# A decoder's last expert layer: gathered rows get buffers of their own, the one-hot rows are made in two blocks, the row maps go ahead of the last shared expert, and an activation table is loaded early

## The chip, the cores and the metric

The kernel runs on one core of a Trainium2 chip. The metric is the time of one execution in device microseconds (us); for each kernel the median of several runs is given. A core has five engines that run beside each other and wait for each other through semaphores: PE (matrix products and transposes), DVE (elementwise work and reductions), ACT (functions and copies), POOL (here mostly the issue of indirect DMAs, which gather or scatter rows by an index), and SP (the issue of plain DMAs). Each engine executes its own list of instructions in order.

## What is computed

The reference is a two-layer decoder on 1024 tokens of 256 numbers. The first layer is a decayed linear attention, a token-hashed expert layer and a layer that retrieves rows of a table. The second is a block-local attention, a quantised cross attention and an expert layer. Only the last one is touched by the change; it is, shortened:

```python
shared_output = _swiglu(x, shared_w1, shared_w3, shared_w2)
scores = jax.nn.sigmoid(x @ gate_w.T)
_, topk_idx = jax.lax.top_k(scores + bias, 2)              # 2 of 16 experts
sel = jnp.take_along_axis(scores, topk_idx, axis=1)
combine = jnp.zeros((T, E)).at[jnp.arange(T)[:, None], topk_idx].add(sel / sel.sum(-1, keepdims=True))
for e in range(E):
    y = _swiglu(x, w1[e], w3[e], w2[e])                    # silu(x w1') * (x w3') w2', inner size 176
    routed_output = routed_output + combine[:, e:e + 1] * y
x = x + shared_output + routed_output                      # x in the experts is layernorm(x)
```

## The kernel before, in words

The tokens lie in eight tiles of 128. Everything up to the row maps is written as Python generators ("streams") that a small planner, `Clock.weave` (lines 117 to 148), interleaves. A stream yields the engine that it needs next; the planner keeps an estimated free time per engine and takes the stream that could start first, where a stream's `lead` is subtracted from that start. `fork` (line 150) starts sub-streams with the lead of their parent. What comes out is one fixed order on each of PE, ACT and DVE. POOL's and SP's orders, and everything after line 1326, are set by the framework's own scheduler. Because a planner's helper records every operation, all of these have line 77 in the profile and are told apart by the names of their tiles.

The last layer is handled tile by tile by `route` (line 1142): layernorm, gate logits, the two best experts of each token as one-hot rows `oh`, and `rank`, each token's position among the tokens of its expert. The normalised rows are stored to DRAM as `xs` (line 366). For the last tile, number 7, line 1177 forks three sub-streams:

- `maps` (line 1234) works out, for up to 31 slots of 128 rows, which token row each slot row gathers (`smap`), where its result goes (`rmap`), and which expert the slot belongs to (`te`). It counts slots with a scan, builds `cols`, and then 16 times makes a 128x128 one-hot block `ohs` on DVE (lines 1275 and 1276, four buffers) and multiplies it with a slice of `cols` on PE (line 1278), all into one accumulator `pmap`. After that come `part0`, `rmap`, `smap`, then `past`, `tef`, `te`, then `none` and a last correction of `rmap`.
- `gates` (line 1182), five small DVE instructions, gives the weights `gsel` that are used at the very end.
- `shared` (line 1194) is the shared expert of tile 7: two products with `s13` (PE), tanh (ACT), two products (DVE, `hd6`), transposes (PE), copies (ACT, `hT6`), two products with `s2` (PE), and the sum into `x7` (DVE).

Then the pools of those streams are closed, a pool `work_c` is opened in the same memory (line 1329), and `run` (line 1377) goes over 24 slots, with 7 more only if they are used. For slot i, `up` (line 1338) loads the expert's number from `te` into a register of PE, gathers 128 rows of `xs` by `smap` with an indirect DMA into `xr` (four buffers of `work_c`, line 1342), transposes them on PE (`tpx`), copies to `xrT` on DVE, makes `ph` on PE (two products of 128x352, in four passes), Silu on ACT and a product on DVE (`hd`). `down` (line 1359) transposes `hd` (`tph`), copies it (`hT`, one part on ACT and one on DVE), makes `py` on PE, copies it to `yr` on ACT, and scatters the rows to `ys` in DRAM (line 1372). The end reads `ys` back, weighs and adds (lines 1394 to 1400).

Two more places matter. `free` (line 864) closes the first layer's pools and opens in their memory the pool `w2` (routed weights, and the maps) and above it `wb2` and `work2` (the last layer's small weights and work tiles). And the loads of those weights (`w_wp` to `w_w2b`, lines 870 to 878) stand in SP's list among the loads `hb` (line 676) that feed the table retrieval.

Of the kernel before, what the change touches and what calls it, by code (L numbers as in the profile page):

```python
# [11 lines left out]
F32 = mybir.dt.float32  # L12
BF16 = mybir.dt.bfloat16
I32 = mybir.dt.int32
U32 = mybir.dt.uint32
U8 = mybir.dt.uint8
AF = mybir.ActivationFunctionType
ALU = mybir.AluOpType
AX = mybir.AxisListType
PSUM = bass.MemoryType.PSUM  # L20

P = 128
D = 256
NT = 8
# [14 lines left out]
NE, EI = 16, 176  # L39
NSL = 2 * NT + NE - 1  # L40
# [4 lines left out]
def bc(ap, axis, n):  # L45

    shape = list(ap.shape)
    shape.insert(axis, n)
    return ap.unsqueeze(axis).to_broadcast(shape)


class Clock:
# [94 lines left out]
                s.done = self.end  # L147
            s.t = self.end + self.HOP * (s.wait[0] != self.last)

    def fork(self, *gens):  # L150

        made = [Stream(g, self.lead, self.end + self.HOP, self.rank) for g in gens]
        self.live.extend(made)
        yield "vector", lambda: max(s.done for s in made) if all(s.done is not None for s in made) else None

# [49 lines left out]
def decoder(ctx, tc, a, out):  # L205
# [3 lines left out]
    ck = Clock(nc)  # L209
# [7 lines left out]
    A = SimpleNamespace(turned=None, freed=None)  # L217
# [646 lines left out]
    def free():  # L864

        yield "vector", lambda: None if fronts_left or A.turned is None else max(A.turned, *known.values())
        front_ctx.close()
        w2 = ctx.enter_context(tc.tile_pool(name="w2", bufs=1))
        wb = work_ctx.enter_context(tc.tile_pool(name="wb2", bufs=1))
        A.wp = load(wb, "wp", [P, 2, D], rows("wp"))  # L870
        A.bp_b = load(wb, "bp", [P, D], a["bp"].to_broadcast([P, D]))
        A.gate = load(wb, "gate", [P, 2, NE], rows("gate"))
        A.gbias = load(wb, "gbias", [P, NE], a["gbias"].to_broadcast([P, NE]))
        A.s13 = load(wb, "s13", [P, 2, 2 * EI], rows("s13"))
        A.s2a = load(wb, "s2a", [P, D], a["s2"][0:P, :])
        A.s2b = load(wb, "s2b", [EH, D], a["s2"][P:EI, :])
        A.w2a = load(w2, "w2a", [P, NE, D], a["w2"][:, 0:P, :].rearrange("e p n -> p e n"))
        A.w2b = load(w2, "w2b", [EH, NE, D], a["w2"][:, P:EI, :].rearrange("e p n -> p e n"))
        A.work2 = work_ctx.enter_context(tc.tile_pool(name="work2", bufs=1))
        A.w2 = w2  # L880
        A.one16 = A.work2.tile([P, NE], F32, name="one16", tag="one16")
        nc.vector.memset(A.one16, 1.0)
        A.spare = A.work2.tile([P, NSL], F32, name="spare", tag="spare")
        nc.gpsimd.iota(A.spare, pattern=[[P, NSL]], base=2 * (P + T), channel_multiplier=1,
                       allow_small_or_imprecise_dtypes=True)
        A.ohr = A.work2.tile([P, NT, 2, NE], F32, name="ohr", tag="ohr")
        A.freed = ck.end
        yield "vector", None
# [253 lines left out]
    def route(*tiles):  # L1142
        work = A.work2
        n, t0 = len(tiles), tiles[0]
        xnT = work.tile([P, 2, n * P], F32, name="xnT6", tag="xnT6")
        yield from layernorm_T(work, "r", tiles, xnT, store=xs)
        pl = yield from bank.take([P, n, NE])
        for i in range(n):
            for k in range(2):
                te_.matmul(pl[:, i, :], xnT[:, k, i * P:(i + 1) * P], A.gate[:, k, :], start=(k == 0), stop=(k == 1))  # L1150
        yield "scalar", None
        sg = work.tile([P, n, NE], F32, name="sg", tag="sg")
        se_.activation(sg, pl, AF.Exp, scale=-1.0)
        bank.give(pl)
        yield "vector", None
        ve_.tensor_scalar(sg, sg, 1.0, None, ALU.add)
        ve_.reciprocal(sg, sg)
        rt = work.tile([P, n, NE], F32, name="rt", tag="rt")
        ve_.tensor_tensor(rt, sg, bc(A.gbias, 1, n), ALU.add)
        for i, t in enumerate(tiles):  # L1160
            m8 = work.tile([P, 8], F32, name="m8", tag="m8", bufs=2)
            ve_.max(m8, rt[:, i])
            i8 = work.tile([P, 8], U32, name="i8", tag="i8", bufs=2)
            ve_.max_index(i8, m8, rt[:, i])
            ve_.tensor_tensor(oh[:, t], bc(i8[:, 0:2], 2, NE), bc(iota16, 1, 2), ALU.is_equal)
            ve_.tensor_tensor(took[:, t, :], oh[:, t, 0, :], oh[:, t, 1, :], ALU.add)
            ve_.tensor_tensor(prior[:, t + 1, :], prior[:, t, :], took[:, t, :], ALU.add)
            yield "tensor", None
        prk = yield from bank.take([P, n, NE])
        for i, t in enumerate(tiles):  # L1170
            te_.matmul(prk[:, i, :], lower, took[:, t, :], start=True, stop=False)
            te_.matmul(prk[:, i, :], ones, prior[:, t, :], start=False, stop=True)
        yield "scalar", None
        se_.copy(rank[:, t0:t0 + n, :], prk)
        bank.give(prk)
        if t0 + n == NT:
            yield from ck.fork(maps(), gates(tiles, sg), shared(tiles, xnT))
        else:
            yield from gates(tiles, sg)
            yield from shared(tiles, xnT)  # L1180

    def gates(tiles, sg):
        work, n, t0 = A.work2, len(tiles), tiles[0]
        yield "vector", None
        sw = work.tile([P, n, 2, NE], F32, name="sw", tag="sw")
        gs = gsel[:, t0:t0 + n, :]
        ve_.tensor_tensor(sw, oh[:, t0:t0 + n], bc(sg, 2, 2), ALU.mult)
        ve_.tensor_reduce(gs, sw, AX.X, ALU.add)
        ws = work.tile([P, n, 1], F32, name="ws", tag="ws")
        ve_.tensor_tensor(ws, gs[:, :, 0:1], gs[:, :, 1:2], ALU.add)  # L1190
        ve_.reciprocal(ws, ws)
        ve_.tensor_tensor(gs, gs, ws.to_broadcast([P, n, 2]), ALU.mult)
# [41 lines left out]
    def maps():  # L1234
# [33 lines left out]
        ve_.tensor_tensor(cols[:, :, 0, :], bc(placef[:, 1, :], 2, NSL), bc(iotat, 1, NT * 2), ALU.is_equal)  # L1268
        ve_.tensor_tensor(cols[:, :, 1, :], cols[:, :, 0, :], bc(tilen, 2, NSL), ALU.mult)
        ve_.tensor_tensor(cols[:, :, 0, :], cols[:, :, 0, :], bc(rown, 2, NSL), ALU.mult)  # L1270
        yield "tensor", None
        pmap = yield from bank.take([P, 2, NSL])
        for tj in range(NT * 2):
            yield "vector", None
            ohs = work.tile([P, P], BF16, name="ohs", tag="ohs", bufs=4)
            ve_.tensor_scalar(ohs, iotar, placef[:, 0, tj:tj + 1], None, ALU.is_equal)
            yield "tensor", None
            te_.matmul(pmap.rearrange("p o n -> p (o n)"), ohs, cols[:, tj].rearrange("p o n -> p (o n)"),
                       start=(tj == 0), stop=(tj == NT * 2 - 1))
        yield "scalar", None  # L1280
        part0 = work.tile([P, NSL], F32, name="part0", tag="part0")
        se_.copy(part0, pmap[:, 0, :])
# [3 lines left out]
        bank.give(pmap)  # L1286
        A.smap = keep.tile([P, NSL], I32, name="smap", tag="smap")
        ve_.tensor_scalar(A.smap, A.rmap, 1, T - 1, ALU.logical_shift_right, ALU.bitwise_and)
        past = work.tile([P, NSL, NE], F32, name="past", tag="past")
        ve_.tensor_tensor(past, bc(iotat, 2, NE), bc(last, 1, NSL), ALU.is_ge)  # L1290
        tef = work.tile([P, NSL], F32, name="tef", tag="tef")
        ve_.tensor_reduce(tef, past, AX.X, ALU.add)
        A.te = keep.tile([P, NSL], I32, name="te", tag="te")
        ve_.tensor_scalar(A.te, tef, float(NE - 1), None, ALU.min)
        none = work.tile([P, NSL], F32, name="none", tag="none")
        ve_.scalar_tensor_tensor(none, A.rmap, 0.0, A.spare, ALU.is_equal, ALU.mult)
        ve_.tensor_tensor(A.rmap, A.rmap, none, ALU.add)
# [40 lines left out]
    def up(i):  # L1338

        e = nc.values_load(te[0:1, i:i + 1], engines=[mybir.EngineType.PE], min_val=0, max_val=NE - 1,  # L1340
                           skip_runtime_bounds_check_because="a count, limited to the last expert above")
        xr = work.tile([P, D], F32, name="xr", tag="xr", bufs=4)
        nc.gpsimd.indirect_dma_start(out=xr, out_offset=None, in_=xs,  # L1343
                                     in_offset=bass.IndirectOffsetOnAxis(ap=smap[:, i:i + 1], axis=0))
        tpx = ps.tile([P, 2, P], F32, name="tpx", tag="tp")
        for k in range(2):
            nc.tensor.transpose(tpx[:, k, :], xr[:, k * P:(k + 1) * P], ident)
        xrT = work.tile([P, 2, P], F32, name="xrT", tag="xrT")
        nc.vector.tensor_copy(xrT, tpx)  # L1349
        ph = ps.tile([P, 2, EI], F32, name="ph", tag="ph")  # L1350
        for k in range(2):
            nc.tensor.matmul(ph.rearrange("p j n -> p (j n)"), xrT[:, k, :], w13[:, bass.ds(e, 1), k, :],  # L1352
                             start=(k == 0), stop=(k == 1))
        hd = work.tile([P, EI], F32, name="hd", tag="hd")
        nc.scalar.activation(hd, ph[:, 0, :], AF.Silu)  # L1355
        nc.vector.tensor_tensor(hd, hd, ph[:, 1, :], ALU.mult)  # L1356
        return e, hd
# [113 lines left out]
```

## Time and profile before

| | |
|---|---|
| runs | 1129.31, 1130.32, 1131.31 us; median 1130.32 us |
| the profiled execution | 1137.11 us, of which the profile's span is 1135.4 us |
| mean granted PE clock in it | 0.734 of full speed |
| PE / DVE / ACT / POOL busy in the span | 823.8 / 819.0 / 515.9 / 576.1 us |
| last `route` tile's layernorm begins | 1007.3 us |
| first gather of the routed stage starts | 1031.9 us |
| first `ph` starts, last `py` ends | 1037.4 us, 1117.8 us |
| end | 1135.4 us |

A row of the timeline gives start, duration, engine, source line, operation, output and inputs with their sizes, how many instructions are merged, and in brackets how long the engine had been idle before it and what ended that. PEld is the loading of PE's stationary operand, which overlaps products. The chain of waits is followed back from the last instruction: each piece has its start, its duration and what it is; "issue" is time that the profile cannot put down to a wait. A row of stages gives, for each stretch of time, the busy time of each engine with its number of instructions, then the PE clock that was granted (1.00 is full speed), the DMA share and GB/s.

### The profile page before, as it was taken

How to read it: one execution, taken by the hardware profiler on the slowest of the kernel's cores; microseconds unless marked ns; L12 is line 12 of the kernel's file. 1: busy time of each engine (PE TensorE's matmuls, PEld its weight loads, DVE VectorE, ACT ScalarE, POOL GpSimd, SP SyncE). 2: the span in 40 equal slices, each digit the busy share in tenths (PEclk: the TensorE clock that was granted, in tenths of full speed). 3: DMA queues.
4: the chain of work that ended last, by engine and by line, in shares of the span. 5: the costliest groups of instructions: out<-in, count | busy, mean ns of one | idle time of the engine just before them, and what ended most of it. 6: DMA issues, size and time to landing. Idle time of an engine off the chain costs nothing.

```text
span 1135.4 us, 15530 instructions
## 1 busy us (share of the span) xinstructions
PE 823.8 (73%) x4945; PEld 505.9 (45%) x4945; DVE 819.0 (72%) x2440; ACT 515.9 (45%) x1039; POOL 576.1 (51%) x597
## 2 busy tenths in 40 slices
PE   4771587926943986767887888887887896746993
PEld 3561465704631674334544445444543453323551
DVE  5459877698779768998789768888688767553223
ACT  2231232502411254544777638676467785731221
POOL 2000767575777577777666747777473000003551
PEclk9786678957975997556667658667757676556997
DMA  6001666685776677679866656667563600001223
GB/s 221 1 5 38 166 168 168 166 246 151 189 202 176 167 196 205 183 189 291 212 173 177 198 153 177 178 186 201 135 190 101 213 1 6 1 5 47 78 76 135
DMA packets 65711, 163.75 MB, mean 144 GB/s; under 512 B 14890, under 2 KB 28571, under 8 KB 65628
## 3 DMA queue, kind: packets, MB, share of 16 engines
q0 software_dynamic: 35072, 106.99, 33.8%
q1 hardware_dynamic: 29404, 54.18, 17.3%
q10 hardware_dynamic: 1152, 1.57, 0.4%
q8 instruction: 40, 0.66, 0.2%
q14 instruction: 43, 0.35, 0.1%
HBM read 156.93 MB, written 5.77 MB: 143 GB/s over the span
## 4 chain that ended last, share of the span: by engine, by line
PE 28%; DVE 21%; ACT 9%; DMA 7%; issue 6%; POOL 5%; SPq 0%; DVEq 0%; POOLq 0%; ACTq 0%
PE bank L77 20%; PE accs L77 5%; DMA g<-in_table,idxT 5%; DVE mx L77 4%; POOL g L77 4%; ACT qqT L77 3%; ACT e L77 3%; DVE g L77 3%; DVE z L77 3%; PE ph L1352 2%; DVE pr L77 1%; DVE oh L77 1%; POOL ys L1372 1%; DMA ys<-yr,rmap 1%; DVE nb L77 1%
## 5 line engine op out<-in xcount | busy, mean ns | idle before, releaser
L77 POOL DMA_INDIRECT g<-in_table,idxT x512 | 521.0, 1018 | 334.7 <-issue 141.4
L77 DVE TENSOR_REDUCE mx<-bank 128x1 f32<-128x1024 f32 x128 | 155.8, 1218 | 48.7 <-PE bank L77 48.3
L77 ACT ACTIVATE e<-bank,nb,qs_q 128x1024 uint8<-128x1024 f32 x128 | 154.5, 1207 | 46.0 <-DVE nb L77 29.6
L77 PE MATMUL accs<-g,blk 128*32 128x256 f32 x1024 | 96.8, 512 | 79.1 <-DVE blk L77 73.6
L77 ACT CAST qqT<-bank 128x1024 bf16<-128x1024 uint8 x128 | 127.6, 1010 | 42.7 <-PE bank L77 42.4
L77 PE MATMUL bank<-kT,qT 64*128 64x512 bf16 x256 | 103.4, 513 | 22.0 <-ACT e L77 19.2
L1343 POOL DMA_INDIRECT xr<-xs,smap x24 | 23.3, 970 | 178.9 <-DVE used L77 166.9
L77 PEld LDWEIGHTS accs<-g,blk 128*32 128x32 f32 x1024 | 32.6, 135 | 126.3 <-DVE blk L77 87.6
L77 PE MATMUL bank<-ident,e 128*128 128x128 f32 x256 | 72.8, 386 | 16.1 <-ACT e L77 11.3
L77 DVE TENSOR_TENSOR g<-g,hb 128x1024 f32<-128x1024 f32 x64 | 78.2, 1222 | 8.2 <-DMA g<-in_table,idxT 6.1
L77 DVE TENSOR_REDUCE z<-g 128x8 f32<-128x1024 f32 x64 | 78.1, 1220 | 2.2
L77 PEld LDWEIGHTS <-qqT 128*128 128x128 bf16 x1024 | 39.8, 103 | 78.0 <-ACT qqT L77 56.2
L77 PE MATMUL accs<-vi,qqT 128*128 128x16 bf16 x1024 | 47.4, 175 | 30.1 <-ACT qqT L77 29.5
L77 PEld LDWEIGHTS bank<-ident,e 128*128 128x128 f32 x256 | 36.3, 185 | 67.9 <-issue 29.4
L77 ACT ACTIVATE th<-u 128x16 f32<-128x16 f32 x64 | 13.9, 217 | 96.4 <-DVE u L77 90.5
L77 PE MATMUL bank<-ident,ln_xn 128*128 128x128 f32 x96 | 24.2, 368 | 32.3 <-ACT ln_xn L77 18.7
L77 ACT ACTIVATE ln_xn<-x,ln_nmr,ln_rstd 128x256 f32<-128x256 f32 x48 | 27.0, 595 | 41.8 <-DVE ln_nmr L77 41.8
L1356 DVE TENSOR_TENSOR hd<-hd,ph 128x176 f32<-128x176 f32 x24 | 8.0, 338 | 49.7 <-ACT hd L1355 49.7
L1352 PE MATMUL ph<-w,xrT 128*128 x96 | 37.7, 513 | 0.8 <-DVE xrT L1349 0.8
L77 DVE TENSOR_SCALAR nb<-mx,nsq,ln 128x1 f32<-128x1 f32 x128 | 34.9, 273 | 4.6
L1372 POOL DMA_INDIRECT ys<-yr,rmap x24 | 23.2, 967 | 29.1 <-ACT yr L1371 23.4
L77 PEld LDWEIGHTS <-qT 64*128 64x128 bf16 x256 | 16.8, 101 | 42.6 <-issue 36.7
(293 smaller groups left out, 1695.0 us busy)
## 6 DMA issues: line engine op xcount, KB each, us to landing
hb<-hdram SPq DMA_DIRECT2D x128, 256.0 KB
g<-in_table,idxT POOLq DMA_INDIRECT x512
w<-in_w SPq DMA_DIRECT2D x16, 352.0 KB
w_w2a<-in_w SPq DMA_DIRECT2D x1, 2048.0 KB
x<-in_x SPq DMA_DIRECT2D x8, 128.0 KB
w_ctxT<-in_ctxT SPq DMA_DIRECT2D x1, 1024.0 KB
w_w_up<-in_w_up SPq DMA_DIRECT2D x1, 1024.0 KB
xs<-ln_xn SPq DMA_DIRECT2D x8, 128.0 KB
```

What stands on the lines that cost most here:

```text
L77: return emit(*args, **kw)
L1343: nc.gpsimd.indirect_dma_start(out=xr, out_offset=None, in_=xs, in_offset=bass.IndirectOffsetOnAxis(ap=smap[:, i:i + 1], axis=0))
L1352: nc.tensor.matmul(ph.rearrange("p j n -> p (j n)"), xrT[:, k, :], w13[:, bass.ds(e, 1), k, :], start=(k == 0), stop=(k == 1))
L1356: nc.vector.tensor_tensor(hd, hd, ph[:, 1, :], ALU.mult)
L1372: put = nc.gpsimd.indirect_dma_start(out=ys, out_offset=bass.IndirectOffsetOnAxis(ap=rmap[:, i:i + 1], axis=0), in_=yr, in_offset=None)
```

## The change

Five edits, all in the last layer:

1. `xr` is no longer a tile of `work_c` with four buffers: three tiles `xr0` to `xr2` are made in pool `w2` when it is opened, and slot i uses number i % 3. Pool `w2` so grows by 3 KB per partition, and `wb2` and `work2` lie higher by as much.
2. `ohs` is made in two blocks of eight, with eight buffers: the streams hand over to the planner once per block, not before every `ohs` and every product.
3. `fork` takes an `ahead` for each sub-stream; `maps` gets 4.0 more lead than `gates` and `shared`.
4. `past`, `tef` and `te` move in front of `part0`, `rmap` and `smap`.
5. A Silu on one column of `part0` is added after `smap`; its result is used by nobody.

```diff
-    def fork(self, *gens):
+    def fork(self, *gens, ahead=None):
 
-        made = [Stream(g, self.lead, self.end + self.HOP, self.rank) for g in gens]
+        made = [Stream(g, self.lead + d, self.end + self.HOP, self.rank) for g, d in zip(gens, ahead or [0.0] * len(gens))]
...
         A.w2 = w2
+        A.xr = [w2.tile([P, D], F32, name=f"xr{i}", tag=f"xr{i}") for i in range(3)]
...
-            yield from ck.fork(maps(), gates(tiles, sg), shared(tiles, xnT))
+            yield from ck.fork(maps(), gates(tiles, sg), shared(tiles, xnT), ahead=(4.0, 0.0, 0.0))
...
-        yield "tensor", None
-        pmap = yield from bank.take([P, 2, NSL])
-        for tj in range(NT * 2):
-            yield "vector", None
-            ohs = work.tile([P, P], BF16, name="ohs", tag="ohs", bufs=4)
-            ve_.tensor_scalar(ohs, iotar, placef[:, 0, tj:tj + 1], None, ALU.is_equal)
+        pmap = None
+        for t0 in (0, NT):
+            ohs = [work.tile([P, P], BF16, name="ohs", tag="ohs", bufs=NT) for _ in range(NT)]
+            for j in range(NT):
+                ve_.tensor_scalar(ohs[j], iotar, placef[:, 0, t0 + j:t0 + j + 1], None, ALU.is_equal)
             yield "tensor", None
-            te_.matmul(pmap.rearrange("p o n -> p (o n)"), ohs, cols[:, tj].rearrange("p o n -> p (o n)"),
-                       start=(tj == 0), stop=(tj == NT * 2 - 1))
+            if pmap is None:
+                pmap = yield from bank.take([P, 2, NSL])
+            for j in range(NT):
+                te_.matmul(pmap.rearrange("p o n -> p (o n)"), ohs[j], cols[:, t0 + j].rearrange("p o n -> p (o n)"),
+                           start=(t0 + j == 0), stop=(t0 + j == NT * 2 - 1))
+            yield "vector", None
...
+        past = work.tile([P, NSL, NE], F32, name="past", tag="past")
+        ve_.tensor_tensor(past, bc(iotat, 2, NE), bc(last, 1, NSL), ALU.is_ge)
...
...
         A.smap = keep.tile([P, NSL], I32, name="smap", tag="smap")
         ve_.tensor_scalar(A.smap, A.rmap, 1, T - 1, ALU.logical_shift_right, ALU.bitwise_and)
-        past = work.tile([P, NSL, NE], F32, name="past", tag="past")
-        ve_.tensor_tensor(past, bc(iotat, 2, NE), bc(last, 1, NSL), ALU.is_ge)
...
+
+        se_.activation(part0[:, 0:1], part0[:, 0:1], AF.Silu)
         none = work.tile([P, NSL], F32, name="none", tag="none")
...
-        xr = work.tile([P, D], F32, name="xr", tag="xr", bufs=4)
+        xr = A.xr[i % 3]
```

What the built programs' instruction lists show: up to the last `route` tile PE, ACT and DVE have the same order in both kernels. From there on DVE does `maps` without a break up to the last `rmap`, then `gates`, then the products of `shared`; PE does all 16 `ohs` products before the products of `shared`. The first gather waits on DVE for `smap` and no longer for the corrected `rmap`. The first transposes `tpx` wait on DVE for `x7`, the end of `shared`. In the routed loop the scheduler orders PE anew. Before, it goes slot by slot from slot 7 on: `ph(i)`, `tph(i-1)`, `tpx(i+1)`, `py(i-1)`, and then `ph(i+1)`. After, slots 2 to 9 go in pairs (`tph`, two slots' `tpx`, `py`, `ph`, `tph`, half a `ph`, `py`, the other half), and from slot 10 on it is `ph(i)`, `py(i-1)`, `tpx(i+1)`, `tph(i)`, the load of the next expert's number, and then `ph(i+1)`. On SP the loads `w_wp` to `w_s2b` stand 14 `hb` loads earlier than before. The fourth gather now waits for the transposes of the first.

More of the change, by code (lines that the diff above doesn't have):

```diff
@@ L1270, in maps @@
         ve_.tensor_tensor(cols[:, :, 0, :], cols[:, :, 0, :], bc(rown, 2, NSL), ALU.mult)
-        yield "tensor", None
-        pmap = yield from bank.take([P, 2, NSL])
-        for tj in range(NT * 2):
-            yield "vector", None
-            ohs = work.tile([P, P], BF16, name="ohs", tag="ohs", bufs=4)
-            ve_.tensor_scalar(ohs, iotar, placef[:, 0, tj:tj + 1], None, ALU.is_equal)
-            yield "tensor", None
-            te_.matmul(pmap.rearrange("p o n -> p (o n)"), ohs, cols[:, tj].rearrange("p o n -> p (o n)"),
-                       start=(tj == 0), stop=(tj == NT * 2 - 1))
+        pmap = None
[3 more added lines that the diff above has]
+                ve_.tensor_scalar(ohs[j], iotar, placef[:, 0, t0 + j:t0 + j + 1], None, ALU.is_equal)
+            yield "tensor", None
+            if pmap is None:
[3 more added lines that the diff above has]
+                           start=(t0 + j == 0), stop=(t0 + j == NT * 2 - 1))
+            yield "vector", None
+        past = work.tile([P, NSL, NE], F32, name="past", tag="past")
+        ve_.tensor_tensor(past, bc(iotat, 2, NE), bc(last, 1, NSL), ALU.is_ge)
+        tef = work.tile([P, NSL], F32, name="tef", tag="tef")
+        ve_.tensor_reduce(tef, past, AX.X, ALU.add)
+        A.te = keep.tile([P, NSL], I32, name="te", tag="te")
+        ve_.tensor_scalar(A.te, tef, float(NE - 1), None, ALU.min)
         yield "scalar", None
@@ L1288, in maps @@
         ve_.tensor_scalar(A.smap, A.rmap, 1, T - 1, ALU.logical_shift_right, ALU.bitwise_and)
-        past = work.tile([P, NSL, NE], F32, name="past", tag="past")
-        ve_.tensor_tensor(past, bc(iotat, 2, NE), bc(last, 1, NSL), ALU.is_ge)
[L1291 to L1294, printed above, removed]
+        se_.activation(part0[:, 0:1], part0[:, 0:1], AF.Silu)
         none = work.tile([P, NSL], F32, name="none", tag="none")
```

## The prediction

> **What bounds the kernel now.** All that the change reorders lies after 1007 us, between the last tile's layernorm and the end, so I read the chain of waits from there on first.
>
> ```profile
> 1022.30 0.70 PE bank L77 x2
> ...
> 1023.35 2.38 PE bank L77 x4
> ...
> 1026.09 0.26 DVE ohs L77
> ...
> 1026.39 2.20 PE bank L77 x13
> 1028.60 0.02 issue
> 1028.62 0.19 ACT part L77
> ...
> 1029.24 0.59 DVE past L77
> ...
> 1031.90 3.14 DMA xr<-xs,smap
> ...
> 1037.37 5.03 PE ph L1352 x8
> ```
>
> Line by line: transposes and `s2` products of the shared expert (0.70, 2.38), three `ohs` earlier and thirteen behind it (2.20), the maps, the first gather (3.14), and the first two `ph` in 5.03. So the shared expert's products stand on PE in front of the maps' products, and everything routed waits for the maps. Next, the page's group of the gathers, with what ended POOL's idle time:
>
> ```profile
> L1343 POOL DMA_INDIRECT xr<-xs,smap x24 | 23.3, 970 | 178.9 <-DVE used L77 166.9
> ```
>
> POOL waited for DVE's maps, mostly once; 24 gathers of 0.97 us are no bound. Then the timeline of one late slot:
>
> ```profile
> 1066.50 1.45 PE L1352 MATMUL ph<-w,xrT 128*128 x4
> 1067.79 0.27 PE L1362 MATMUL tph<-ident,hd 128*128 128x128 f32 x1
> 1068.01 0.38 PE L1347 MATMUL tpx<-ident,xr 128*128 128x128 f32 x2
> 1068.21 0.27 ACT L1365 COPY hT<-tph 128x128 f32<-128x128 f32 x1
> 1068.53 0.70 PE L1368 MATMUL py<-w_w2a,hT 128*128 x2
> 1068.80 0.41 DVE L1349 COPY xrT<-tpx 128x256 f32<-128x256 f32 x1
> 1069.78 0.56 PE L1352 MATMUL ph<-w,xrT 128*128 x1
> ```
>
> PE carries the loop: `ph` for 1.29 (to 1067.79), two `tph` 0.22, `tpx` 0.38, a wait of some 0.2 for ACT's `hT` (to 1068.48), and `py` 1.25 (to 1069.78). That is 3.28 per slot; from `ph(7)` at 1059.94 to `ph(23)` at 1112.42 it holds for all 16. Last, stages with the granted clock (the column behind POOL) around the loop's start:
>
> ```profile
> 1039.00:1041.00 2.00, 2.00 (x4) 1.03 (x4) 0.00 (x0) 0.79 (x1) 0.11 (x1) 0.50 0.29 82
> 1043.00:1045.00 2.00, 1.63 (x9) 1.04 (x8) 1.38 (x5) 0.27 (x1) 1.62 (x2) 1.00 0.15 29
> ```
>
> **A. Maps before the shared expert: the start of the loop.** Today DVE runs the five gate operations (0.99) among the maps; `cols` ends at 1021.63. Without them the maps' first link, `nti`, moves from 1016.17 to about 1015.6 (pcn's product ends 1015.57): 0.57 earlier, `cols` at 1021.06. Sixteen `ohs` at 0.169 (2.20/13) are 2.71: 1023.77, and PE's last product 0.29 later, 1024.06, where it was 1028.58. `past`, `tef`, `te` (1.59 today) now fill DVE while PE finishes, so `smap` is at about 1025.8. The first gather today started 0.84 after the corrected `rmap`; it will wait for `smap` alone: issue at 1026.6, landed 1029.7, where it was 1035.04. That is 5.3 earlier.
>
> But the shared expert now stands behind the `ohs` products on PE, and the first `tpx` behind it. Its first product (2.69 today) ends at 1026.75, tanh at 1027.12; on DVE the maps end at 1026.2, the gates (0.99) at 1027.2, `hd` (0.71) at 1027.9; transposes 0.74, `hT` 0.31, `s2` 0.05 + 2.37, `x7` 0.47: 1031.9. So `tpx(0)` starts at 1031.9, not at 1029.7 + 0.3, where today it is at 1035.34: **-3.4**. Of the gather's 5.3, about 1.9 end as a wait on the shared expert. Today `ph(0)` came 1.41 behind the release of `tpx(1)`, because the expert's number is loaded to PE's register after that wait for the second gather; with both gathers landed, about 0.5 of this is gone: **-3.9** at `ph(0)`.
>
> **B. The table load, and the other things that cost nothing.**
>
> ```profile
> 1040.21 1.28 ACT L1355 ACT_TABLE_LOAD   x1 [11.40 <-PE ph L1352]
> ```
>
> ACT had idled 11.40 and PE was in `ph(1)` until 1042.40; the Silu went at 1041.50 and its result was wanted only after `ph(1)`. The Trainium skill, "ScalarE: Activation LUTs", section "What ACT_TABLE_LOAD costs", puts a switch at 1.28 plus a drain of 1.38, so 2.66. By the page an early load would be worth up to 2.66 if it stood on the chain; by the row 1.28, and here neither is on it: `ph(1)` covers it. The cover would be too short only if `ph(1)` ran at the full clock (some 1.3 instead of 2.5), where the early load would save up to 0.5. I take 0. The new load lies behind `part`, ahead of the shared expert's tanh; ACT's list has no second load, tanh being in the same set. It ends at about 1026, before that product ends at 1026.75: cover 0.7; without it tanh, and the chain, would be up to 0.7 later.
>
> Three buffers for four: the fourth gather now waits for `tpx(0)` and lands 3.14 + about 1 later, near 1036, while it is wanted behind the first two `ph` (5.03), about 1038.5: nothing. Later a gather has three periods (10 us) for 3.14 + 0.98: nothing. The seven weight loads moved on SP ahead of 14 `hb` loads: SP stands there until a product ending at 426.7, and the next `hb` issue is at 433.9; seven issues are about 3.5, inside that gap of 7.2. Without the gap the retrieval would come up to 3.5 later. The first of them that needs freed memory inherits SP's wait of 8.7 at 508.77 from `w_wp`: nothing new. Two blocks of `ohs`: eight buffers take away the returns to the planner, the work is the same and is counted above.
>
> **C. The clock.** It is 0.50 from 971 to 1042 and 1.00 after, and the first two `ph` take 5.03 for that reason. The skill, "TensorE: Matmul & The Clock Gate", "Part 1: The HAM clock gate", lets the clock rise after one busy window of about 3.4 us whose phase runs freely. By that rule, a busy `ohs` and shared stretch (about 7 us without DVE between) could lift it before `ph(0)`: 5.03 becomes about 2.6, a gain of up to 2.5. By the row, today's stretch of the same work, 1021 to 1029, did not, and a window at 971 to 974.4 with 0.09 idle did not either; the switches in this trace (923.3, 943.7, 967.55, 970.95, 1042.35) lie on a grid of 3.41, so a loop starting 3.9 earlier meets it at another phase: up to 0.9 longer cold. Value taken: 0; ends -2.5 and +0.9.
>
> **D. Slots 2 to 9.** PE takes these in pairs. From the end of `ph(1)` to `ph(10)` today: 27.38. With rows of today's durations, a pair is 6.05, and the whole is 27.07: **-0.3**, estimated.
>
> **E. Slots 10 to 22.** The order on PE is now `ph(i)`, `py(i-1)`, `tpx(i+1)`, `tph(i)`, register load, `ph(i+1)`. The wait for ACT's `hT` (0.2 to 0.27) vanishes: `hT(i-1)` is made during `ph(i)`. What is late next is `xrT(i+1)`: today `py` (1.25) ran while DVE made it (0.41), now only `tph` (0.22) does. So 1.29 + 1.25 + 0.38 + 0.04 + 0.41 + 0.05 = 3.42 at most, 3.40 at least (part of `tpx` ends under the copy's issue), against 3.28: +0.12 to +0.14, 13 times: **+1.6**. Queued behind `ph(i+1)`'s wait are `py(i)` and `tpx(i+2)`, so the delay is passed on from slot to slot. POOL (0.98 + 0.96 per slot) is still free.
>
> **F. The end.** `py` no longer has a slot's work behind the last `ph`: from `ph(23)` to the last `py`'s end 4.68 by the rows, today 1117.84 - 1112.42 = 5.42: **-0.7**. Scatter, read back and sum follow unchanged.
>
> **Sum.** -3.9 - 0.3 + 1.6 - 0.7 = -3.3. On the profiled execution, 1137.11 becomes 1133.8 (span 1135.4 to 1132.1); that execution was 6.8 above the median, and what lies between is not in the part changed, so the difference carries to the median: 1130.32 - 3.3 = **1127.0**.
>
> **Rivals.** (a) The sum as it stands, 1127.0, within about 1.2: chance 0.48.
>
> (b) The new order costs nothing: `xrT` comes in time, or `tpx` starts under `py`, and the period is 3.28. Then E is 0: 1125.4. For it: PE's rows overlap at their ends by 0.1 to 0.2. Against: `tpx` stands behind `py` in the list. 0.15.
>
> (c) The clock rises before the first `ph`: about -2.2 more, 1124.8. For and against as in C. 0.12.
>
> (d) The start yields less: the planner's list has DVE finish all maps before `hd`, and each hand-over that I took at 0.02 to 0.05 is a guess over a dozen links; with 0.9 colder, and a period of 3.45, the sum is -3.9 + 0.9 - 0.3 + 2.2 + 0.3 - 0.7, about -1.5: 1128.8. 0.17.
>
> (e) Slower: the register load. Today it sits behind the second `py` wait and is over 0.90 after that wait's end (DVE's `hT` 1068.88, `ph`'s weights 1069.78), partly under `py`. Now it stands behind `tph`'s wait for `hd`, some 0.73 after `ph`'s end, and `ph(i+1)` waits for it. `xrT` is ready 2.1 after `ph`'s end, so up to about 1.4 the load is hidden. The first slot's distance of 1.41 is an upper end that sits on that point, 0.90 the lower. If it takes 1.8 under load (dispatch queued behind `py`), the period is 3.83, thirteen slots cost 7.2 in place of 1.6, and the sum is +2.3: 1132.6; slower than before by over 0.2% from there on. I take 0.9, the row of this very place. 0.08.
>
> **How the numbers follow.** A measurement of this kernel tells 0.2% (2.26 us) from no change: faster is below 1128.06, slower above 1132.58. Of (a) about five sixths lies below (0.40), (b) and (c) wholly (0.27), (d) hardly: faster 0.67, and I give 0.04 of it back for the many guessed hand-overs: 0.63. Of (e) and of mishaps of (d) 0.09 are slower; same 0.28. Range: (c)'s lower part leaves some 0.08 below 1124.0, (e) and the end of (d) some 0.11 above 1130.2.
>
> **What would show it.** Right, if the chain has all `ohs` products ending near 1024, the first gather landing near 1030, and `tpx(0)` released by DVE's `x`, 3 to 4 earlier than before; if late slots are 3.40 apart with PE's idle time before `ph` ended by `xrT`; and if ACT's table load moves to about 1025 with no other gap closed. Wrong, if the clock changes at another place than with the second `ph`, if the late period is 3.28 or above 3.6, or if anything before 1007 moves.

## The result and the profile after

Over 22 runs each, the changed kernel takes 1128.66 us (median), the kernel before 1131.37 us: ratio 0.9976, 95% interval 0.9969 to 0.9984, so 1.8 to 3.5 us faster. The forecast was 1127.0 from 1130.32, a ratio of 0.9971. The changed kernel's profiled execution took 1127.84 us, with a span of 1126.1 us.

The spans of the two profiled executions differ by 9.3 us, but 6.3 of that lie ahead of the change: the last tile's final `prior` add starts at 1015.18 us in the one and at 1008.86 us in the other. In the last four kernels of the table of experiments it starts at 1007.3 to 1009.5. The profiled execution of before was 6.8 above the median of its first three runs, and its table retrieval's last gather ends at 865.0, where the five other profiles of this speed have 856.2 to 859.3; so I take these 6.3 as a matter of that one execution. All stage times below are therefore counted from that add, called T. The first eight experiments of the table below ran where every kernel, that of before too, took 1250 to 1330 us and the retrieval's last gather ended only at 1002 to 1049, so they are read from T on and not by their whole times.

| from T, us | before | changed | difference by the prediction's times | measured |
|---|---|---|---|---|
| `cols` ends | 6.45 | 5.89 | -0.57 | -0.56 |
| `smap` ends | 14.06 | 10.29 | -3.4 | -3.77 |
| first gather starts | 16.72 | 10.56 | -5.3 | -6.16 |
| `x7` ends | 11.00 | 16.31 | +5.7 | +5.31 |
| `tpx(0)` starts | 20.16 | 16.37 | -3.4 | -3.79 |
| `ph(0)` starts | 22.19 | 18.33 | -3.9 | -3.86 |
| `ph(0)` to `ph(10)` | 32.41 | 32.03 | -0.3 | -0.38 |
| `ph(10)` to `ph(23)` | 42.64 | 44.11 | +1.6 | +1.47 |
| `ph(23)` to the end of the last `py` | 5.42 | 4.56 | -0.7 | -0.86 |
| from there to the end | 17.56 | 18.21 | 0 | +0.65 |
| sum | 120.22 | 117.24 | -3.3 | -2.98 |

The changed kernel's chain of waits, from the maps to the loop (start, duration, what):

```profile
1014.96 5.20 PE bank L77 x20
1020.18 0.33 ACT th L77
...
1021.30 0.70 PE bank L77 x2
...
1022.34 2.38 PE bank L77 x4
1024.75 0.43 DVE x L77
1025.23 0.70 PE tpx L1353 x2
...
1027.19 5.03 PE ph L1358 x8
```

All sixteen `ohs` products and the shared expert's first product are now one stretch of PE (5.20), and the shared expert goes on down to `x7`, which releases `tpx`. The gather, 3.14 long in the chain of before, is not in it any more. The page's group of the gathers:

```profile
L1349 POOL DMA_INDIRECT xr<-xs,smap x24 | 23.3, 969 | 186.2 <-DVE none L77 161.8
```

The profile puts the end of POOL's long idle time down to `none`, the step behind `smap`, and no longer to `used` at the end of the maps; the instruction list names `smap`. A late slot in the timeline:

```profile
1066.01 1.45 PE L1358 MATMUL ph<-w,xrT 128*128 x4 [0.30 <-DVE xrT L1355]
1067.29 0.59 PE L1374 MATMUL py<-w_w2a,hT 128*128 x2
1067.82 0.70 PE L1375 MATMUL py<-w_w2b,hT 48*128 x2
1068.44 0.44 PE L1353 MATMUL tpx<-ident,xr 128*128 128x128 f32 x2
1068.72 0.27 PE L1368 MATMUL tph<-ident,hd 128*128 128x128 f32 x1
1068.92 0.42 DVE L1355 COPY xrT<-tpx 128x256 f32<-128x256 f32 x1 [0.74 <-PE tpx L1353]
1069.40 1.45 PE L1358 MATMUL ph<-w,xrT 128*128 x4 [0.30 <-DVE xrT L1355]
```

Between two `ph` lie 3.39 us, and each time PE idles 0.30 until DVE's `xrT`. The wait of before for ACT's `hT` (0.14 in the slot that the prediction shows) is gone, and this one stands in its place. The table load has moved, with nothing waiting behind it:

```profile
1017.87 1.28 ACT L77 ACT_TABLE_LOAD   x1
```

And the clock (the column behind POOL's busy time) stays at 0.50 past the end of the second `ph` (1032.22). First a row of before, whose second `ph` ends at 1042.40, then two of the changed kernel:

```profile
1042.00:1043.00 1.00, 1.00 (x5) 0.59 (x3) 0.16 (x1) 0.32 (x1) 0.00 (x0) 0.68 0.00 0
```

```profile
1032.00:1033.00 1.00, 1.00 (x6) 0.94 (x5) 0.36 (x2) 0.58 (x2) 0.00 (x0) 0.54 0.00 0
1033.00:1034.00 1.00, 1.00 (x7) 0.61 (x5) 0.92 (x3) 0.00 (x0) 0.66 (x1) 1.00 0.00 0
```

A mean of 0.68 between 0.50 and 1.00 puts the rise at 1042.64, one of 0.54 at 1032.92: 0.24 behind the end of the second `ph` before, 0.70 now. Counted from the start of `ph(0)`, the clock rose after 5.27 us before and after 5.73 now.

### The profile page after: what moved, and what is told of

Read it like the earlier page. It is cut to its first block, busy times and chain, and to the rows that moved or that the text cites. A ratio compares the mean times of both kernels' runs of the same rounds, so it can differ in the third digit from the quotient of the medians.

```text
span 1126.1 us, 15533 instructions
## 1 busy us (share of the span) xinstructions
PE 808.8 (72%) x4945; PEld 498.3 (44%) x4945; DVE 821.0 (73%) x2440; ACT 517.7 (46%) x1040; POOL 571.6 (51%) x597
## 5 line engine op out<-in xcount | busy, mean ns | idle before, releaser
L77 PE MATMUL bank<-w_ctxT,aT 128*128 128x256 f32 x128 | 32.8, 407 | 3.9 <-DVE aT L77 2.6
```

Source lines behind the costliest of these rows:

```text
L77: return emit(*args, **kw)
```

## The experiments

The theory: the start gains because maps no longer stand behind the shared expert and the gates, and because the gathers are not held by memory; the rest of the gather's lead is lost on the shared expert; the loop loses because `tpx` stands behind `py`; the table load is worth nothing. Rivals: one edit carries all, or the table load does, or another wait sets the slot.

From T on, the same stage repeats to 0.03 us from one execution to the next (`x7` ends at 16.30 to 16.33 in all seven profiles with the changed kernel's start). The ratios of the first eight kernels are taken over whole executions, in whose profiles T lies anywhere from 1152.6 to 1204.1. Those of four (no_early_silu to xr_only) are above 1 by more than their intervals, although from T to the end three of these kernels are earlier than before and xr_only is 0.6 later. There is no profile of before beside them, so what made their whole times longer stays open.

| from T, us | `tpx(0)` | `ph(0)` | last `py` ends | end | ratio to before (95%) |
|---|---|---|---|---|---|
| before | 20.16 | 22.19 | 102.66 | 120.22 | |
| changed | 16.37 | 18.33 | 99.03 | 117.24 | 0.9976 (0.9969 to 0.9984) |
| no_early_silu | 16.36 | 18.33 | 98.29 | 116.27 | 1.0047 (1.0002 to 1.0093) |
| no_ahead | 17.64 | 20.41 | 101.05 | 119.06 | 1.0145 (1.0036 to 1.0254) |
| xr_in_work_c | 19.94 | 22.17 | 101.04 | 119.26 | 1.0128 (1.0043 to 1.0213) |
| xr_only | 17.78 | 20.44 | 103.06 | 120.81 | 1.0175 (1.0102 to 1.0248) |
| shared_out | 13.84 | 16.65 | 97.50 | 116.24 | one run |
| hole | 13.28 | 15.92 | 96.51 | 114.51 | 0.9870 (0.9789 to 0.9952) |
| hand_loop | 16.38 | 17.68 | 91.89 | 110.30 | 0.9826 (0.9746 to 0.9906) |
| hand_loop_no_silu | 16.36 | 17.67 | 94.69 | 113.17 | 0.9942 (0.9910 to 0.9974) |
| hand_py_first | 16.35 | 17.65 | 100.79 | 119.24 | 0.9983 (0.9963 to 1.0002) |
| warm | 16.36 | 18.32 | 97.46 | 115.96 | 0.9969 (0.9951 to 0.9986) |
| hole_hand | 13.17 | 14.45 | 86.38 | 105.45 | 0.9872 (0.9847 to 0.9898) |
| hole_hand_warm | 13.27 | 14.54 | 86.43 | 105.12 | 0.9881 (0.9853 to 0.9909) |

What follows the last `py` (scatter, read back, sum) takes 17.6 to 19.1 us from profile to profile without any kernel touching it; the changed kernel's 0.65 there is inside that spread, and "last `py` ends" is the better measure.

**Edit 1 out: `xr` in `work_c` again** (xr_in_work_c).

```diff
-        xr = A.xr[i % 3]
+        xr = work.tile([P, D], F32, name="xr", tag="xr", bufs=4)
```

> The changed kernel without edit 1 (xr again four buffers of work_c; edits 2 to 5 stay). My theory: without buffers of its own the gather waits for what lived in that memory, the shared expert's x7 among it; x7 is done 16.3 us behind the last prior add, so the first gather starts at 16.8, lands at 19.9 and tpx(0) comes at 20.2, as before: the start's gain is gone, ratio 1.000 to 1.001. Rival (the memory holds nothing back, the order of maps and shared is all): tpx(0) at 16.4, ratio 0.9976.

Its timeline, the first gather:

```profile
1213.92 0.42 DVE L77 SCALAR_TENSOR_TENSOR x<-bank,x 128x256 f32<-128x256 f32 x1 [3.51 <-PE bank L77]
1214.64 0.94 POOL L1348 DMA_INDIRECT xr<-xs,smap  x1 [171.11 <-DVE x L77]
```

The gather waits for `x7`, 6.3 us after `smap`. `tpx(0)` is at 19.94: the start's gain is gone, as expected. Without buffers of its own, putting maps ahead is worth nothing at the start. The last `py` is still 1.6 earlier than before: this list keeps slots in pairs up to slot 13, a pair takes 5.97 (4.46 and 1.51 from `ph` to `ph`), and from `ph(0)` to the last `py` it takes 78.87 (80.46 before, 80.70 in the changed kernel).

**Edit 1 alone** (xr_only), on the kernel before:

```diff
         A.w2 = w2
+        A.xr = [w2.tile([P, D], F32, name=f"xr{i}", tag=f"xr{i}") for i in range(3)]
...
-        xr = work.tile([P, D], F32, name="xr", tag="xr", bufs=4)
+        xr = A.xr[i % 3]
```

> The kernel before with edit 1 alone (xr in three buffers of its own). My theory: the first gather no longer waits for the corrected rmap but for smap (14.06 us behind the last prior add), starts at 14.5 instead of 16.7 and tpx(0) comes at 18.0 instead of 20.2: -2.2 us; the built loop has the new order from slot 5 on, +0.11 us on some 18 slots, and a shorter end (-0.9): total -1.2 us, ratio about 0.999. Rival 1 (the waits for memory don't matter): start unchanged, loop +2, ratio 1.001. Rival 2 (own buffers give all): ratio 0.9976.

`tpx(0)` comes at 17.78, near the 18.0 expected: the wait for `used` was the memory's. But the whole is not faster, as I had expected, but slower: the last `py` ends 0.40 later than before. From `ph(0)` to there it takes 82.62, 2.15 more than before, since this list has the new order from slot 5 on. I had put 1.0 on that. The start's gain is smaller at `ph(0)`, too: it is 2.66 behind `tpx(0)` (2.03 before). The second gather is issued 1.43 behind the first (1.25 before), which makes 0.2 of it; the rest is not attributed.

**Edit 3 out: no lead for maps** (no_ahead).

```diff
-            yield from ck.fork(maps(), gates(tiles, sg), shared(tiles, xnT), ahead=(4.0, 0.0, 0.0))
+            yield from ck.fork(maps(), gates(tiles, sg), shared(tiles, xnT))
```

> The changed kernel without edit 3 (maps get no extra lead): the built list has gates in front of the maps again, the shared expert's first product in front of the ohs, its hd and its second products between the two blocks. My theory (the order of maps against shared sets the start): second block of products behind s2, past, tef and te in front of smap, so smap 14.5 us and tpx(0) about 18.4 us behind the last prior add, against 16.4 in the changed kernel and 20.2 before: half of the start's gain, ratio about 0.9993. Rival 1 (the lead carries all): tpx(0) at 20.2, ratio 1.000 to 1.001. Rival 2 (the blocks and own buffers carry all): tpx(0) at 16.4, ratio 0.9976.

`smap` ends at 14.10 and `tpx(0)` is at 17.64, 1.3 behind the changed kernel. I had expected 18.4: the second eight products, with their `ohs` all made, took 0.59 and not DVE's pace of 0.169 each. The last `py` ends at 101.05. So buffers of its own alone gain 2.4 at `tpx(0)` (xr_only), edits 2, 4 and 5 without the lead only 0.1 more, and the lead another 1.3 (2.1 at `ph(0)`). Neither edit 1 nor edit 3 carries all; edits 2 and 4 were not taken out one by one.

**Edit 5 out: no early Silu** (no_early_silu).

```diff
-        se_.activation(part0[:, 0:1], part0[:, 0:1], AF.Silu)
```

> The changed kernel without edit 5 (the early Silu). My theory: the table load goes back in front of the first hd and is hidden under ph(1), so it costs nothing; tpx(0) stays 16.4 us behind the last tile's prior add (16.37 in the changed kernel, 20.16 before); the scheduler falls back to the earlier order of the loop, with 3.28 us per late slot instead of 3.39 but a longer end, together -0.2 us. Total within 0.5 us of the changed kernel, ratio to before 0.997 to 0.998. Rival (the early table load is itself worth something): 1.3 to 2.7 us slower than the changed kernel, ratio to before 0.9987 to 1.000.

The start is the same to 0.01. The table load is back in front of the first `hd`:

```profile
1222.46 5.03 PE L1356 MATMUL ph<-w,xrT 128*128 x8 [0.85 <-DVE xrT L1353]
...
1225.29 1.28 ACT L1359 ACT_TABLE_LOAD   x1 [7.58 <-PE ph L1356]
```

It ends at 1226.57, before `ph(1)` (1227.49), and costs nothing. From `ph(0)` to the last `py` it takes 79.96 instead of 80.70, 0.74 less where 0.2 was expected: the early Silu is not worth 1.3 here, it costs 0.74, because that one ACT instruction turned the scheduler to the order with the longer slot.

**The shared expert of the last tile left out** (shared_out).

```diff
-            yield from ck.fork(maps(), gates(tiles, sg), shared(tiles, xnT), ahead=(4.0, 0.0, 0.0))
+            yield from ck.fork(maps(), gates(tiles, sg), ahead=(4.0, 0.0))
```

> The changed kernel with the last tile's shared expert left out (its contribution is missing from x7). My theory: tpx(0) waits for the shared expert alone, so without it it follows the first gather's landing, 10.6 + 3.1 + 0.3 = 14.0 us behind the last prior add instead of 16.4. Rival (another wait stands there too, pools or registers): it stays near 16.

```profile
1173.60 1.48 PE L1353 MATMUL tpx<-ident,xr 128*128 128x128 f32 x4 [5.06 <-DMA xr<-xs,smap]
```

`tpx(0)` is released by the gather and comes at 13.84, 2.5 earlier: that is the part of the gather's lead that the change loses to the shared expert (forecast: 1.9). Of it 1.7 reach `ph(0)`, which now waits for the second gather.

**The shared expert in PE's idle time** (hole). PE idles 5.7 us for the first `ohs`. Here `shared`'s first product and tanh stand there, `hd` right behind the last `ohs`.

```diff
-            yield from ck.fork(maps(), gates(tiles, sg), shared(tiles, xnT), ahead=(4.0, 0.0, 0.0))
+            yield from maps(tiles, sg, xnT)
...
         te_.matmul(pcn, ones, prior[:, NT, :], start=True, stop=True)
...
+        for k in range(2):
+            te_.matmul(ph7.rearrange("p j n -> p (j n)"), xnT[:, k, 0:P], A.s13[:, k, :], start=(k == 0), stop=(k == 1))
...
+        se_.activation(th, ph7[:, 0, :], AF.Tanh, scale=0.5)
...
+        ve_.scalar_tensor_tensor(hd, th, 1.0, ph7[:, 0, :], ALU.add, ALU.mult)
+        ve_.tensor_tensor(hd, hd, ph7[:, 1, :], ALU.mult)
```

Behind that come, in this order, `part0`, `rmap` and `smap`, the shared expert's `hT6` and `s2` products, `past`, `tef`, `te`, `none`, `x7` and the gates.

> The changed kernel with the last tile's streams written in one fixed order: the shared expert's first product and tanh run in PE's idle time in front of the ohs products, its hd right behind the last ohs on DVE, past, tef and te behind smap, gates last. My theory (the shared expert behind the ohs is what bounds the start): x7 at 13.3 us and tpx(0) at 13.4 us behind the last prior add, 3 us earlier than in the changed kernel; the built loop is the earlier order (3.28 us a slot), so the last py ends near 96 us (99.0 in the changed kernel), end near 114. Rival (the gather's landing is the bound, or DVE): tpx(0) at 15 or later, gain under 1.4 us.

`x7` ends at 13.04, `tpx(0)` is at 13.28, the last `py` ends at 96.51: as expected, the shared expert was the bound, and it need not be. More could hardly be had from it: the first gather starts at 9.71, and in hole_hand below, where it starts at 9.70, it has landed at 13.08.

**The loop's order by hand** (hand_loop). The loop stands inside the framework's manual order for PE, ACT and DVE:

```diff
-            nxt = up(i)
-            if held is not None:
-                down(i - 1, *held)
-            held = nxt
...
+        with tc.manual_schedule(engines={PE, mybir.EngineType.Activation, mybir.EngineType.DVE}):
+            e, xrT = turn(lo)
...
+                hd = make(e, xrT)
+                e0 = e
+                if i + 1 < hi:
+                    e, xrT = turn(i + 1)
+                if held is not None:
+                    down(i - 1, *held)
+                held = e0, back(hd)
```

`turn` holds the register load, the gather, `tpx` and `xrT`; `make` `ph` and `hd`; `back` `tph` and `hT`; `down` `py`, `yr` and the scatter.

> The changed kernel with the routed loop's order on PE, ACT and DVE written by hand: ph(i), tpx(i+1), py(i-1), tph(i), and the next expert's number loaded in front of tpx. Nothing else differs. My theory (in the changed kernel ph waits for xrT because only tph lies between, so the order of PE alone costs the 0.25 us): xrT is made under py, no wait is left and a slot takes PE's own 1.29 + 0.38 + 1.25 + 0.22 = 3.14 us instead of 3.39; the last py ends 95 to 96 us behind the last prior add (99.0 in the changed kernel, 102.7 before). Rival (the chain hd, tph, hT of ACT and DVE, or the register load, sets the slot): 3.3 us or more a slot, last py at 98 or later.

The last `py` ends at 91.89, 7.1 earlier than in the changed kernel. A slot takes 2.83, less than the 3.14 that I had added up. A slot of the undisturbed loop (from hole_hand, below):

```profile
1050.89 0.89 PEld L1382 LDWEIGHTS ph<-w,xrT 128*128 128x128 f32 x4
1051.00 1.35 PE L1382 MATMUL ph<-w,xrT 128*128 x4
...
1052.19 0.38 PE L1374 MATMUL tpx<-ident,xr 128*128 128x128 f32 x2
...
1052.41 0.60 PE L1400 MATMUL py<-w_w2a,hT 128*128 x2
...
1052.93 0.70 PE L1401 MATMUL py<-w_w2b,hT 48*128 x2
...
1053.56 0.33 PE L1391 MATMUL tph<-ident,hd 128*128 128x128 f32 x1
...
1053.84 1.35 PE L1382 MATMUL ph<-w,xrT 128*128 x4
```

From start to start `ph` takes 1.19, `tpx` 0.22, `py` 1.15 and `tph` 0.28, where I had 1.29, 0.38, 1.25 and 0.22. The 0.38 was the length of the `tpx` row, which runs on beside the next product. The 0.10 each of `ph` and `py` is in their first product, and goes with its weight load: here the load begins 0.11 ahead of the product, in the late slot of before together with it:

```profile
1066.50 0.89 PEld L1352 LDWEIGHTS ph<-w,xrT 128*128 128x128 f32 x4 [0.33 <-issue]
```

In hand_loop five slots were 0.3 to 1.0 longer, mostly where ACT's `hT` or `hd` came late with no cause that the profile shows. Late slots of this kind stand only in profiles of the first eight experiments, those with the longer retrieval; in hole_hand there are none. What makes them stays open.

**The same, with `py` in front of `tpx`** (hand_py_first):

```diff
-                if i + 1 < hi:
-                    e, xrT = turn(i + 1)
                 if held is not None:
                     down(i - 1, *held)
+                if i + 1 < hi:
+                    e, xrT = turn(i + 1)
```

> The hand-written loop with one step moved: py(i-1) in front of tpx(i+1), which is the changed kernel's order of its late slots, now in all slots. My theory (this order alone makes ph wait for xrT): 3.39 us a slot instead of 2.83, the last py 22 x 0.56 = 12.3 us later than in the hand-written loop, about 104 us behind the last prior add. Rival (the 3.39 came from the register load or from three buffers): 2.83 us a slot, last py at 92.

From `ph(1)` on a slot takes 3.39 to 3.40, with the changed kernel's wait:

```profile
1056.19 1.45 PE L1362 MATMUL ph<-w,xrT 128*128 x4 [0.30 <-DVE xrT L1356]
```

So the order of `py` and `tpx` makes it. The three buffers are the same in hand_loop; the register load moves along with `tpx`, but PE has no other wait in these slots than that for `xrT`. The last `py` ends at 100.79 and not at 104: hand_loop, on which I had counted, had lost some 3 us in those five slots.

**The hand-written loop without the early Silu** (hand_loop_no_silu), one line taken out of hand_loop. The page in its expectation is the one on table loads that part B of the prediction names.

```diff
-        se_.activation(part0[:, 0:1], part0[:, 0:1], AF.Silu)
```

> The hand-written loop without the early Silu. The orders of PE, ACT and DVE are the same but for the place of the table load. My theory: in this loop tph(0) stands in front of ph(1), so ph(1) no longer covers the load, which waits for ph(0): ph(1) and all behind it come 1.28 us later than with the early Silu. By the page's price (load and drain) 2.66 us later. Rival (it is hidden here too): 0.

Its ACT, and its `tph(0)`, then `tph(0)` of hand_loop:

```profile
1175.03 1.28 ACT L1363 ACT_TABLE_LOAD   x1 [6.92 <-PE ph L1360]
1176.33 0.32 ACT L1363 ACTIVATE hd<-ph 128x176 f32<-128x176 f32 x1
...
1177.07 0.33 PE L1369 MATMUL tph<-ident,hd 128*128 128x128 f32 x1 [1.76 <-DVE hd L1364]
```

```profile
1173.88 0.33 PE L1371 MATMUL tph<-ident,hd 128*128 128x128 f32 x1 [0.48 <-DVE hd L1366]
```

PE's wait for `hd` grows from 0.48 to 1.76, by 1.28: the load's own duration. Where `tph(0)` stands in front of `ph(1)`, the cover is gone and the early load is worth that, and not the 2.66 that the Trainium skill ("ScalarE: Activation LUTs", "What ACT_TABLE_LOAD costs") gives with its drain. The other 1.5 us by which the last `py` is later are a balance of late slots: two in a row took 5.01 and 4.59 instead of 2.83, with the clock down to 0.50 in the second, and three of hand_loop's five did not come.

**PE kept busy, to lift the clock** (warm): the shared expert's first product twice more, result used by nobody. The page's rule, here and in hole_hand_warm, is that of the clock in part C of the prediction.

```diff
         te_.matmul(pcn, ones, prior[:, NT, :], start=True, stop=True)
+        warm = yield from bank.take([P, 2, EI])
+        for k in range(4):
+            nc.tensor.matmul(warm.rearrange("p j n -> p (j n)"), A.xnT7[:, k % 2, 0:P], A.s13[:, k % 2, :], start=(k % 2 == 0), stop=(k % 2 == 1))
+        bank.give(warm)
```

> The changed kernel with two more runs of the shared expert's first product (four matmuls, result used by nobody) on PE while it waits for the ohs, from 9 to 15 us... counted from the last tile's layernorm: about 0.4 to 5.8 us behind the last prior add. Theory by the page's rule (one full window of 3.4 us of work lifts the clock): 1.00 from about 5 us behind the prior add; shared expert's products and the first two ph take half, tpx(0) at 13.5 instead of 16.4, first two ph 2.5 instead of 5.03. Theory by the rows of before (the stretch did not lift it): clock 0.50 until the second ph, tpx(0) 16.4.

```profile
1007.60:1011.00 3.40, 3.40 (x7) 2.15 (x7) 2.79 (x14) 0.16 (x1) 0.00 (x0) 0.51 0.01 2
1011.00:1014.40 3.40, 1.81 (x9) 0.77 (x7) 3.30 (x12) 0.00 (x0) 0.00 (x0) 0.99 0.00 0
1014.40:1017.80 3.40, 3.40 (x14) 2.14 (x14) 3.26 (x16) 1.62 (x3) 0.00 (x0) 0.50 0.02 5
```

Neither expectation holds. One window of full work did lift the clock, as the Trainium skill ("TensorE: Matmul & The Clock Gate", "Part 1: The HAM clock gate") says. The extra matmuls then ended sooner (4.27 and not 5.4), PE idled 1.6 until the `ohs`, and after one window with 1.81 busy of 3.40 the clock was back at 0.50. The page has it fall after an idle window; here a half busy one was enough. The third window was full, half of it with `ohs` products at DVE's pace, and did not lift it. So the shared expert ran at 0.50 again, and `tpx(0)` is at 16.36. In its later slots this list has the earlier order (3.28), hence its shorter loop.

**Both together** (hole_hand): the edits of hole and of hand_loop, and

```diff
+        yield from gates(tiles, sg)
         ve_.scalar_tensor_tensor(xt[t7], py, 0.5, xt[t7], ALU.mult, ALU.add)
         bank.give(py)
-        yield from gates(tiles, sg)
```

> Fixed order of the last tile and hand-written loop together, gates moved in front of x7. My theory (start and loop add up): tpx(0) at 13.3 and ph(0) at 14.6 us behind the last prior add, 2.83 us a slot, last py at 88.9 (99.0 in the changed kernel), end about 107; 10 us less than the changed kernel. Rival (gathers are late when the loop starts earlier and runs faster): last py at 91 or later.

`tpx(0)` at 13.17, 2.83 a slot, last `py` at 86.38 (88.9 was expected with hand_loop's late slots in it, and those did not come). Over repeated runs 1117.60 us against 1131.53: ratio 0.9872, 0.9847 to 0.9898, faster than both kernels. In its slots from the third on PE waits for nobody until the last `py`.

**And with one more product for the clock** (hole_hand_warm): behind the product into `ph7`,

```diff
+        for _ in range(1):
+            for k in range(2):
+                te_.matmul(warm.rearrange("p j n -> p (j n)"), xnT[:, k, 0:P], A.s13[:, k, :], start=(k == 0), stop=(k == 1))
```

> The same with one more run of the shared expert's first product in PE's idle time (result used by nobody). By the page's rule on the clock: 1.00 from about 5 us behind the prior add, s2 and transposes half as long, ph(0) 1.3 instead of 2.69, tpx(0) bound by the first gather's landing at 12.9; last py at 87. By the rows of before: as without it, 88.9.

86.43: the same as without. As in warm, the clock was 1.00 for one window (1013.08 to 1016.50, PE busy for 1.83 of it) and then 0.50 again: the extra product ends 1.59 us before the first `ohs`, and what follows takes as long as at 0.50 (`ph(0)` 2.68).

## Why the prediction was right, step by step

**A** was right in its mechanism and nearly in its sizes. Own buffers release the gather (xr_in_work_c), the order releases `smap` (no_ahead), and the shared expert eats the rest (shared_out, hole). The gather came 6.2 earlier, not 5.3: I had given it 0.84 behind its releaser, as in before, and it took 0.27; the rest is `smap`, 0.3 earlier than my sum. That did not count, since `tpx(0)` waits for `x7`. The shared expert took 2.5 of the gather's lead, not 1.9. `x7` came 0.4 earlier than my chain: the shared expert's first product followed the last `ohs` product at once, while I had taken 0.3 more for those to end.

**B**: the load costs nothing on its path, right; it measured 0 with the cover (no_early_silu) and 1.28 without (hand_loop_no_silu). What I did not see is that the added instruction takes part in deciding the loop's order: without it the list falls back to the earlier one. It is no simple rule, since xr_only has the new order without a Silu, and warm the earlier one with it. The three buffers cost nothing: the fourth gather, issued at 1026.19, had 6.2 us until its slot's transposes (1032.44). The moved weight loads show no cost either (last gather of the retrieval at 857.6).

**C**: value taken 0, right in the sum, but not by the whole of its reason. A busy stretch ahead of the loop can lift the clock: in warm a full window of f32 products did. In the changed kernel the stretch behind 1015 is full in the profile (5.20) and did not; its first half is paced by DVE, one short product per 0.17 us, and that this is why is not shown. The clock did rise at another place than with the second `ph`, one of my signs of being wrong: 0.70 behind its end, 0.46 later from `ph(0)` than before, about half of the 0.9 that I had as an end. The rise of before is at 1042.64, not 1042.35.

**D, E and F** were right: -0.38, +1.47 and -0.86 for -0.3, +1.6 and -0.7; a pair took 5.97, for 6.05, and the late period was 3.39, for 3.40 to 3.42. hand_py_first shows the cause of E by itself. The period met my sum partly by luck: `py` took 1.15 and not 1.25, as its weights were loaded ahead, and the transposes `tpx` 0.44 and not 0.38. The pieces of the slot before (1.29, 0.22, 0.38, 0.2, 1.25) add up to 3.34, not to the 3.28 that I gave for them; the wait was 0.14. The 3.28 stands, as it was read from `ph` to `ph`.

**Rivals.** (b) did not occur: `xrT` does come late. (c) did not either, nor (d) but for its colder start, about half as long as assumed. (e), the register load: in the hand-written loop, where the load stands behind `ph`, it fits a slot of 2.83 without any wait; placed behind `tph`, as in the changed kernel, the profile has PE's idle time end with `xrT`. The 1.41 ahead of the first `ph` was not the load's price in the loop.

The forecast of 3.3 us less became 2.98 in the profiles and 2.71 in the medians. Up to the last `py` it was 3.63; the 0.65 that is lost behind it is not attributed, and without it the sum would have missed to the other side by as much.

## What to carry to other kernels

A step brought forward gains only up to the next thing that stands behind it on the same engine: here the gather came 6.2 us earlier and the loop 3.9, as the shared expert had been pushed behind the maps; PE's idle 5.7 us in front of the maps' products had room for it. When a scheduler orders a loop, look at the order after every edit, even an edit elsewhere: one ACT instruction ahead of the loop changed a slot from 3.28 to 3.39 us, and writing the order by hand (`tpx` in front of `py`, `tph` last) made it 2.83. Put between a transpose and the product that needs its copy the longest work that doesn't depend on it.

## What the runs showed that I had not expected

- A group of products takes 0.10 us less when its first weights are loaded ahead of it: `ph` 1.19 us from start to start instead of 1.29. With that, and without waits, a slot takes 2.83, where I had added up 3.14 from the rows of a loop with waits.
- The order in pairs takes 2.99 a slot (5.97 for two), less than either order of the late slots (3.28 and 3.39). The scheduler had it in slots 2 to 9 and left it.
- The clock can fall quickly: after one window of 3.4 us with PE busy for 1.81 of it (warm). In hand_loop_no_silu a window with 1.77 of 3.41 was followed by 0.50 as well, but one with 1.69, right behind the rise, was not; and a window with 2.93 was enough to lift the clock (hole_hand, 1025.99 to 1029.40), where a full one with `ohs` products in it was not (the changed kernel). What counts as busy, and at what share, stays open.
